# Two graph layers in one kernel: when the second layer's scaled copies and the next batch's preparation are issued

## The chip, the core and the metric

The kernel runs on one core of one Trainium2 chip. The time is the device time of one execution in microseconds (us); several runs are given with their median. One further execution is recorded by the hardware profiler, and all durations below come from that one. PE is the matrix engine (TensorE), PEld its weight loads, DVE is VectorE, ACT is ScalarE, POOL is GpSimd, SP is SyncE, which issues most DMAs.

## The reference

Input `x` is 8 batches of 2048 nodes with 256 features; `adj` is one 2048 x 2048 0/1 matrix for all batches. Two layers run one after the other, each adding to `x`. The change concerns the second:

```python
h = relu(layernorm(x))
q = (h @ W).reshape(B, N, 4, 64)
e_src, e_dst = q . a[:64], q . a[64:]              # per node and head
e = leaky_relu(e_src[:, :, None] + e_dst[:, None, :], 0.2)
attn = softmax(where(adj > 0, e, -9e15), axis=2)   # over the neighbours
x = x + elu(attn @ q)
```

The first layer is multi-head attention under the same mask, with a softmax over each chunk of 256 keys, an output projection and a layer norm. All arithmetic here is in float32.

## The kernel before

One program in five instruction queues, written out in one function, `layers`. Each engine runs its own queue in the order in which the Python code issues to it; semaphores order them against each other, and nothing is rescheduled after that. Small jobs are Python generators: a list `aside` holds them, and `advance()` takes one step from each, until one step gives `None` (a heavy step, one to a call); `True` marks a light step, `False` a wait. `drain(until)` repeats `advance()` until a condition holds.

**The second layer.** A batch has four passes, one for each pair of heads (`hp`) and each half of the 2048 queries (`half`); a pass has 16 rounds, one for each tile of 128 keys (`jt`), so a batch has 64 rounds. Eight batches make 32 passes and 512 rounds. The exponent of the score is taken apart so that no matrix of scores is needed:

- `nears` (L801, ACT), once in a pass: the exponential of the source part for 1024 queries, one tile for each of two heads, into PSUM (`places[0]`, `places[1]`). It reads `es`, fetched by DMA (L593, SP).
- `clipped` (L812, DVE), two instructions a round, one for each head: the larger of near and far part, cut off by the mask, makes a tile `e` of 128 x 1024. `begun` issues it two rounds ahead of its use. Ten `e` tiles exist, two for each of five rounds.
- `weigh_rows` (L823, PE): multiplies `e` by the keys' rows `qn` and adds into `acc`, 8 matmuls a round (the trace shows 16).
- The softmax's denominator takes two key tiles at a time, called pair m here (rounds 2m and 2m+1, m from 0 to 7). In the even round two scaled copies `t` of `e` are made (L926, ACT); in the odd round POOL adds the next `e` onto them (L930), and two rounds later PE sums them (`add_up_rows`, L835) into `den`. The last pair of a pass isn't added by POOL; PE sums `t` and `e` apart, in the same round. Four `t` tiles exist, enough for two pairs.
- At the end of a pass ACT copies `acc` and `den` out (`cT` L935, `dT` L944), and the generator `ending` finishes: PE transposes (`flip`, L156), a reciprocal (L858, DVE), twice a product `z` (L869, DVE), four small ACT instructions (L878 to L881), two POOL adds (L883, L884) and a store.

`den` lies in one half of the PSUM tile `places[2]`; the other half (`aux()`) is the one place in which all small jobs put their PE results.

**The preparation of the next batch** (`preparation`) runs beside the passes of this batch as one more generator: for each of four blocks of 512 nodes it normalises (L144, ACT), transposes (`block_turned`: L156 on PE, the copy `hT` L164 on ACT) and projects onto the two vectors (L620, PE; copy `er` L627, ACT); then come the bounds (L632 to L679 on DVE, ACT and POOL, with two trips through DRAM and some rounds of waiting), and at last eight projections by W (`narrow`, L153, PE, 32 matmuls in the trace for each), each scaled on DVE (L693) into `qn`. Counted by the steps that give `None` there are 21. The passes of the next batch need it, and a `drain` at round 8 of the fourth pass makes sure that it is done.

The order of one round before the change:

```python
ready.append(begun(*rounds[s + 2]))   # nears, if a pass begins there; then e
weigh_rows(jt, hp, now, qn, acc)
# even jt: the two copies t; odd jt: POOL's adds; jt 15: cT
# the sums that are due; jt 15: dT, and ending is put ahead of the others
if jt != NKT - 3:
    advance()
```

## Time and profile before

| | us |
|---|---|
| median of three runs | 4279.99 (4279.74 to 4282.05) |
| the profiled execution: its time | 4285.06 |
| its span, first to last instruction | 4283.3 |
| first `e` of the second layer (L812) | 2761.0 from the start |
| last `e` of the second layer | 4259.1 from the start |
| one L812 / L930 / L926 / L869 | 1.275 / 2.388 / 1.142 / 0.680 |
| granted TensorE clock, mean | 0.993 |

The spans are those of one execution; an instruction's mean comes from its group of equal instructions. Matmuls overlap each other, and their ends are modelled, so the time from the start of one to the start of the next says more of PE than its busy share. A wait in brackets at the end of a line is idle time of the engine just before that instruction, with the instruction that ended it.

### The profile page before, as it was taken

The page shows a single profiled execution, that of the slowest core. Times are in us where ns is not written, and L with a number is a line of the kernel's source. Part 1 is how long each engine was busy: PE and PEld are TensorE (multiplying, and loading weights), DVE is VectorE, ACT ScalarE, POOL GpSimd, SP SyncE. Part 2 cuts the span into 40 slices and gives each one's busy share as a digit, 9 for nine tenths or more (in the row PEclk, how much of TensorE's full clock was granted, in tenths as well). Part 3 has the DMA queues.
Part 4 walks back from the last instruction along what each step waited for, and adds up shares of the span by engine and source line. Part 5 has one row for each costly group of instructions (what it writes and reads, how often), then busy time and mean ns, then how long its engine had stood idle before and what let it go on. Part 6 is the DMA issues. An engine that isn't in the chain of part 4 may idle for free. (4 is left out here: it accounts for less than half of the span.)

```text
span 4283.3 us, 86541 instructions
## 1 busy us (share of the span) xinstructions
PE 4101.6 (96%) x34742; PEld 1478.7 (35%) x34742; DVE 3220.3 (75%) x3974; ACT 2528.9 (59%) x3194; POOL 3411.4 (80%) x1799
## 2 busy tenths in 40 slices
PE   7999999999999999999999989999999999999998
PEld 3333333333333333333333333333333233333322
DVE  5786676766666676666666667789888988888897
ACT  5655565655655555555555557565665656566565
POOL 2577787887887888888788688888788878887897
PEclk9999999999999999999999999999999999999999
DMA  3221111121121111121112122212121211112121
GB/s 110 88 74 56 52 57 52 54 63 46 54 62 47 48 58 57 49 57 59 47 52 59 47 61 61 81 47 67 43 70 35 79 58 57 57 54 70 33 60 36
DMA packets 278730, 248.15 MB, mean 58 GB/s; under 512 B 95792, under 2 KB 228656, under 8 KB 278320
## 3 DMA queue, kind: packets, MB, share of 16 engines
q1 hardware_dynamic: 273136, 223.67, 17.9%
q0 software_dynamic: 5184, 18.88, 1.1%
q8 instruction: 275, 4.51, 0.4%
q14 instruction: 135, 1.11, 0.1%
HBM read 204.15 MB, written 36.18 MB: 56 GB/s over the span
## 5 line engine op out<-in xcount | busy, mean ns | idle before, releaser
L448 DVE SCALAR_TENSOR_TENSOR E<-big,limit 128x1024 f32<-128x1024 f32 x1024 | 1182.2, 1216 | 650.0 <-PE big L440 629.4
L742 POOL TENSOR_TENSOR add<-E 128x1024 f32<-128x1024 f32 x512 | 1203.4, 2372 | 548.2 <-PE both L460 472.2
L454 ACT ACTIVATE E<-E 128x1024 f32<-128x1024 f32 x1024 | 1054.5, 1056 | 535.1 <-DVE E L448 517.1
L812 DVE SCALAR_TENSOR_TENSOR e<-big,far,limit 128x1024 f32<-128x1024 f32 x1024 | 1239.4, 1275 | 37.5 <-POOL t L930 21.0
L930 POOL TENSOR_TENSOR t<-t,e 128x1024 f32<-128x1024 f32 x448 | 1054.6, 2388 | 226.2 <-ACT t L926 219.7
L823 PE MATMUL acc<-e,qn 128*32 128x512 f32 x8192 | 1065.2, 595 | 3.5 <-DVE e L812 3.4
L460 PE MATMUL both<-E,v 128*32 128x512 f32 x8192 | 992.9, 596 | 0.2
L440 PE MATMUL big<-qT,kT 64*128 64x512 f32 x4096 | 964.5, 608 | 28.1 <-DVE E L448 26.5
L926 ACT ACTIVATE t<-e,quot 128x1024 f32<-128x1024 f32 x512 | 562.5, 1142 | 242.4 <-PE big L835 147.5
L440 PEld LDWEIGHTS big<-qT,kT 64*128 64x128 f32 x4096 | 366.0, 187 | 575.3 <-issue 389.5
L500 POOL TENSOR_TENSOR acc<-acc,c 128x1024 f32<-128x1024 f32 x224 | 530.2, 2367 | 1.4 <-DVE c L498 1.4
L460 PEld LDWEIGHTS both<-E,v 128*32 128x32 f32 x8192 | 276.2, 109 | 595.8 <-issue 340.0
L823 PEld LDWEIGHTS acc<-e,qn 128*32 128x32 f32 x8192 | 292.1, 110 | 496.2 <-issue 435.4
L835 PE MATMUL big<-t,for_sums 128*32 128x512 f32 x2048 | 380.3, 596 | 66.7 <-POOL t L930 50.1
L498 DVE TENSOR_TENSOR c<-both,r 128x512 f32<-128x512 f32 x448 | 308.8, 689 | 40.2 <-PE both L460 14.3
L471 PE MATMUL big<-add,ones 128*32 128x512 f32 x2048 | 282.1, 605 | 12.2 <-DVE E L448 1.4
L478 ACT COPY s<-big 128x512 f32<-128x512 f32 x256 | 149.8, 585 | 78.3 <-PE big L471 78.0
L835 PEld LDWEIGHTS big<-t,for_sums 128*32 128x32 f32 x2048 | 80.9, 109 | 279.0 <-POOL t L930 183.3
L153 PE MATMUL big<-w,hT 128*32 128x256 f32 x2048 | 151.1, 380 | 4.1 <-ACT dT L944 4.1
L164 ACT COPY hT<-big 128x512 f32<-128x512 f32 x128 | 74.2, 579 | 132.6 <-PE big L156 132.6
L144 ACT ACTIVATE h<-x,off,rstd 128x256 f32<-128x256 f32 x256 | 139.1, 592 | 14.2 <-DMA x<-x 13.8
L337 ACT ACTIVATE qT<-big,bq 128x512 f32<-128x512 f32 x64 | 43.9, 687 | 148.7 <-PE big L153 148.7
(117 smaller groups left out, 3059.4 us busy)
## 6 DMA issues: line engine op xcount, KB each, us to landing
r<-inv SPq DMA_DIRECT2D x1024, 64.0 KB
x<-in_x_dram SPq DMA_DIRECT2D x96, 512.0 KB
es<-er SPq DMA_DIRECT2D x64, 512.0 KB
adj_in<-in_adj_dram SPq DMA_DIRECT2D x32, 512.0 KB
x<-o POOLq DMA_DIRECT2D x32, 512.0 KB, 3.3
xh<-x SPq DMA_DIRECT2D x64, 256.0 KB
out_dram<-xh SPq DMA_DIRECT2D x64, 256.0 KB
x<-x SPq DMA_DIRECT2D x28, 512.0 KB
```

Of the source, the lines that this page charges most:

```text
L440: nc.tensor.matmul(ps[:, hh, :], ks[kt // NT][own, hp, (kt % NT) * P : (kt % NT + 1) * P], qs[qb][own, hp, :], start=True, stop=True,)
L448: nc.vector.scalar_tensor_tensor(e, ps, -0.5, bcast(limit[:, qb, kt, :], 1, 2), ALU.max, ALU.min)
L454: nc.scalar.activation(e, e, AF.Exp, scale=0.25 * EDGE)
L460: nc.tensor.matmul(both[part][32 * h : 32 * h + 32, :], vs[kt // NT][:, kt % NT, mine], es[h // 2][:, h % 2, :], start=first, stop=not first,)
L498: nc.vector.tensor_tensor(to[:, part, :], both[part], r, ALU.mult)
L500: nc.gpsimd.tensor_tensor(acc, acc, to, ALU.add)
L742: nc.gpsimd.tensor_tensor(both, tiles[0][hp], tiles[1][hp], ALU.add)
L812: nc.vector.scalar_tensor_tensor(e, near[hh], far[:, jt, h : h + 1], limit[:, 2 * half : 2 * half + 2, jt, :], ALU.max, ALU.min,)
L823: nc.tensor.matmul(acc[blk][32 * q : 32 * q + 32, :], qn[jt // NT][:, jt % NT, hp * P + 32 * q : hp * P + 32 * q + 32], es[q // 2][:, blk, :],
L835: nc.tensor.matmul(den[32 * q : 32 * q + 32, :], for_sums[:, m, 2 * hp + q // 2, :], ts[q // 2][:, q % 2, :], start=(m == 0 and k == 0), s ...
L926: nc.scalar.activation(t, now[hh], AF.Copy, scale=quot[:, jt // 2, h : h + 1])
L930: nc.gpsimd.tensor_tensor(ts[hh], ts[hh], now[hh], ALU.add)
```

## The change

Two things change, both in the loop over the second layer's rounds.

The scaled copies move into a function `scaled`, which is called in the odd round for the pair that begins in the next round: after that round's sums (and after `dT` in the last round of a pass) and before `advance()`. The first pair's copies are made ahead of the loop.

The preparation is wrapped in `paced`, which lets a step that gave `None` be followed by the next only when two and a half rounds for each such step have gone by since the preparation began. The `drain` in the fourth pass switches the pacing off.

```diff
+    at, hurry = [0], [False]
+
+    def paced(steps_of):
+
+        first, done = at[0], 0
+        for got in steps_of:
+            yield got
+            if got is None:
+                done += 1
+                while 2 * (at[0] - first) < 5 * done and not hurry[0]:
+                    yield False
...
+    def scaled(k, jt, now):
+
+        b, hp, half = passes[k]
+        quot = shared[b][4]
+        ts = []
+        for hh in range(2):
+            t = heads_tile("t", "q", 4)
+            h = 2 * hp + hh
+            nc.scalar.activation(t, now[hh], AF.Copy, scale=quot[:, jt // 2, h : h + 1])
+            ts.append(t)
+        return ts
...
     ready = [begun(*rounds[0]), begun(*rounds[1])]
+    shares = [scaled(*rounds[0], ready[0])]
...
-        here[0] = len(steps) + s // 4
+        here[0], at[0] = len(steps) + s // 4, s
...
-                aside.append(preparation(b + 1))
+                aside.append(paced(preparation(b + 1)))
...
+            hurry[0] = True
             drain(lambda: b1 in shared)
+            hurry[0] = False
...
         if jt % 2 == 0:
-            ts = []
-            for hh in range(2):
-                t = heads_tile("t", "q", 4)
-                h = 2 * hp + hh
-                nc.scalar.activation(t, now[hh], AF.Copy, scale=quot[:, jt // 2, h : h + 1])
-                ts.append(t)
+            ts = shares.pop()
...
+        if jt % 2 and ready:
+            shares.append(scaled(*rounds[s + 1], ready[0]))

         if jt != NKT - 3:
             advance()
```

## The prediction

> **What bounds the kernel now.** The page first: four engines are all busy, so shares settle nothing.

> ```profile
> PE 4101.6 (96%) x34742; PEld 1478.7 (35%) x34742; DVE 3220.3 (75%) x3974; ACT 2528.9 (59%) x3194; POOL 3411.4 (80%) x1799
> ```

> The diff touches only the second layer, so I cut that into passes by POOL's clock, from the first add (L930) of a pass to the first add of the next: passes 0 to 3 of the fourth batch, then a pass of the last batch, which has no preparation beside it. Columns: stretch, length, then busy PE, PEld, DVE, ACT and POOL.

> ```profile
> 3343.33:3392.92 49.59, 46.09 (x400) 14.81 (x404) 40.44 (x38) 34.34 (x49) 41.49 (x23) 1.00 0.26 79
> 3392.92:3435.62 42.70, 41.45 (x381) 12.63 (x374) 40.85 (x38) 29.66 (x39) 37.96 (x19) 1.00 0.23 55
> 3435.62:3488.54 52.92, 50.79 (x572) 24.06 (x576) 42.80 (x45) 27.37 (x36) 38.48 (x21) 1.00 0.07 21
> 3488.54:3532.32 43.78, 41.87 (x374) 13.24 (x366) 42.70 (x39) 25.94 (x30) 37.96 (x18) 1.00 0.29 82
> 4141.85:4184.47 42.62, 39.92 (x341) 12.31 (x342) 39.85 (x36) 25.95 (x30) 37.88 (x19) 1.00 0.16 51
> ```

> A batch is 189.0 us (the first four rows); the last batch runs at 42.6 a pass. In the last row POOL is busy 37.88 and idle 4.74, nearly all of it one wait, which the timeline at the end of a pass shows.

> ```profile
> 4173.99 2.31 ACT L801 ACTIVATE big<-es,off_s 128x1024 f32<-128x1024 f32 x2 [1.13 <-DVE e L812]
> ...
> 4175.25 0.62 PE L835 MATMUL big<-t,for_sums 128*32 128x512 f32 x2 [0.20 <-POOL t L930]
> ...
> 4182.76 0.58 ACT L944 COPY dT<-big 128x512 f32<-128x512 f32 x1 [2.39 <-PE big L835]
> 4183.24 4.27 ACT L926 ACTIVATE t<-e,quot 128x1024 f32<-128x1024 f32 x4
> ...
> 4184.47 9.43 POOL L930 TENSOR_TENSOR t<-t,e 128x1024 f32<-128x1024 f32 x4 [4.58 <-ACT t L926]
> ...
> 4185.12 0.26 DVE L858 RECIPROCAL inverse<-big 128x16 f32<-128x16 f32 x1 [2.68 <-PE big L156]
> ...
> 4196.34 0.63 ACT L878 ACTIVATE z<-z 128x512 f32<-128x512 f32 x1 [2.18 <-DVE z L869]
> ...
> 4196.46 1.06 PE L835 MATMUL big<-t,for_sums 128*32 128x512 f32 x8 [0.41 <-DVE z L869]
> ...
> 4198.59 2.17 ACT L926 ACTIVATE t<-e,quot 128x1024 f32<-128x1024 f32 x2
> ...
> 4201.14 1.28 POOL L883 TENSOR_TENSOR z<-z 128x512 f32<-128x512 f32 x1
> ```

> The loop that sets 42.6 is POOL's adds (without a break), the PE sums of the last pairs, ACT's copies cT and dT, ACT's first scaled copy, POOL again. DVE has 2.68 us of slack before L858. In passes 0 and 1 the loop is the same: POOL's waits at their ends are 7.62 and 4.58. Pass 2 holds the eight projections (L153, the `qn` steps), and PE sets it: its weighs (L823) start 3.44 apart in a round with a projection where a weigh alone takes 1.72, so a projection costs 1.72; sums (L835) 0.86, four transposes with their turnaround 0.6.

> [...] By start-to-start times PE needs 16 x 1.72 + 9 x 0.86 + 3 x 0.6 = 37.1 of 42.6, so 5 us are free, and I go by those.

> **Part one, copies a round earlier.** No instruction is added; 512 copies (L926, 1.14 each) change place in ACT's queue. A copy writes the `t` tile that pair m-2 held, so it waits for that pair's sums on PE. Before, those sums were issued a round earlier; now they are issued in the same round, just ahead of it, and what follows on ACT waits with it. From the order of the built program, four things follow.

> (a) End of a pass: the copies of pair 7 now stand before the two exponentials (L801) that DVE's next `e` tiles need. Sums of pair 5 resume at 4175.25; elsewhere a copy starts 1.15 after the start of its sums (4208.50 to 4209.65), so second copy 4176.4, exponential 1.05 later at 4177.45, 1.12 long, first `e` of the next pass about 4178.66, not 4175.20: 3.5 late. DVE's slack takes 2.7; six `e` at 1.19 end 4185.9, so L858 and both z (L869) come 0.7 late. POOL's first add waits for the copy behind dT as before, and its `e` is there by 4182.3, two us early: no cost there, and one for one if `e` were later by more than that.

> (b) The second z group (L878 to L881, 1.86 to the end of L880) stood before the copies of pair 3 and now stands behind them. The sums of pair 1 wait for the z in the other half of their PSUM tile (4196.46 above): 4197.16 after. Copies 4198.25 to 4200.4, L880 ends 4202.2, POOL's z 4202.25 instead of 4201.14: POOL stands still 1.1 us a pass. Last batch: 4 x 1.1 = 4.4. [...]

> (c) Passes 0 and 1: the preparation's h and hT (L144 0.59, L164 0.58) now stand behind copies, and PE's transposes, which need them, stand before the next weighs. Pass 0: h of round 5 is ready after sums of pair 1 (end 3358.1) plus copies, z group, two h: 3363.9; PE reaches it at 3359.8 and waits 4.2; two later places (L620 behind an L164 that stands behind copies, and the transposes of round 12) add 0.7 and 1.9. From there to the sums of pair 6 PE needs 10 x 1.72 + 4 x 0.86 + 4 x 0.6 + 0.45 = 23.5, with waits 30.3; POOL needs 27.2, so PE is 3.1 late. Against that, the hT and two h that stood before the first copy of pass 1 (gap 7.62 against 4.58) are gone: -3.0. Pass 0: +0.1, say 0. Pass 1: `e` starts 4.3 before the first add, not 5.8, so (b) becomes 2.6; PE waits 3.1 (L164 behind the second z group) and 1.9 (h behind a copy), and comes 2.3 late to the last sums: +4.9.

> (d) Pass 2: (b) with a lead of 4.6 is 2.3.

> **Part two, pacing.** The order shows what comes of it. Steps counted by weighs before them: projections stood at 40 to 45, 47, 48 and now stand at 45, 47, 48, 51, 52, 54, 55, 56. Transposes move by up to 6 rounds. It is no even spread: fixed waits before the 13th step put it at 42, when the pace is already behind. Nothing is left for the drain at round 56, so no burst; the next passes' loads (L593, SP) are issued at round 56 as before; `x` loads on SP come later by the same few rounds, each still a block of steps ahead of its use. POOL's small L656 and L657 move past z, where DVE's result is ready: 2.06 of wait goes.

> Pass 2 then has two projections before its last sums: two rounds with one need 2 x 1.72 + 0.86 + 1.72 = 6.02 against POOL's two adds 4.78, twice: 2.5 late. 38.5 busy + 4.7 + 2.5 + 0.6 (dT later) + 2.3 (d) = 48.6 for 52.9: -4.3. Pass 3 has six: PE 16 x 1.72 + 9 x 0.86 + 6 x 1.72 + 3 x 0.6 + 1.2 (the first waits for dT) = 48.6 for 43.8: +4.8; POOL's own chain (38 + 4.7 + the z wait) stays inside that.

> Sum per batch: 0 + 4.9 - 4.3 + 4.8 = +5.4. Seven batches have a preparation: 38. The first overlaps the end of layer one, where its PE waits may hide: 0 to 5.4, taken as the others because its passes 2 and 3 get the same order. With 4.4: +42. The profiled execution took 4285.06 (span 4283.3), which becomes 4327; the median of the runs, 4279.99, becomes **4322**.

> **Rivals.** *Faster:* PE's sums are done when ACT reaches the copies. Then (b) and PE's lateness in (c) are nil: pass 0 -3.0, pass 1 0, pass 2 46.3 (-6.6), pass 3 +4.8, so -4.8 x 7 = -34, 4246. For it: POOL's long waits in the second layer are all for a copy (219.7 us), and the 7.62 is cured. Against it: ACT already waits 147.5 us for those sums with a round more in hand. It decides once a copy waits under about a microsecond. *Much slower:* PE sets passes 0 and 1, so its waits count in full (6.8 for 3.1, 5.0 for 2.3): 11.8 a batch, +87, 4367. For it: PE is busy 46.09 of 49.59; against: its sums there wait for POOL. *The pacing does nothing:* pass 2 and 3 keep their old lengths plus 2.3 and 1.1, a batch +8.3, 4342. Against: six of eight projections do leave pass 2. *No change:* POOL's gain at the pass end and the z wait cancel, 4280.

> **How the numbers follow.** Forecast 0.58, much slower or no pacing 0.17, no change 0.07, faster 0.18. About 0.2% (8.6 us) is what a measurement here can tell from nothing. Range 4255 to 4352: down into the faster case, up to between the slower ones. A gain over 8.6 us 0.18, none 0.07, a loss 0.75.

> **What would show it.** The last batch decides (a) and (b) alone: passes of 43.7 instead of 42.6, L883 waiting about 1 us for ACT, the 2.68 before L858 gone and a new DVE wait of 3 to 4 us at L812 for ACT's L801. In pass 1, PE waits at L620 and L156 for ACT's hT and h; pass 2 near 48.6, pass 3 near 48.6. If the last batch stays at 42.6 and passes 2 and 3 add up to under 93, the forecast is wrong and the faster rival holds.

## The result, and the profile after

The changed kernel takes 4348.68 us (median of four runs, 4345.81 to 4350.93) against 4281.02 for the kernel before (4279.74 to 4283.56): a ratio of 1.0157 [1.0139, 1.0175]. The profiled execution took 4345.81 us, 60.8 more than that of before; the medians, over more runs, are 67.7 apart. The copies are L922 now, POOL's adds L952, `cT` L957, `dT` L966; the other lines that matter keep their numbers. First the engine line of the page.

```profile
PE 4107.7 (95%) x34742; PEld 1478.4 (34%) x34742; DVE 3215.8 (74%) x3974; ACT 2524.6 (58%) x3194; POOL 3410.6 (79%) x1799
```

The counts are those of before and the busy times nearly so: no work was added, so all that was lost is waiting. Next the four passes of the fourth batch and one of the last batch, cut by POOL's first add as before (stretch, length, busy PE, PEld, DVE, ACT, POOL, then the granted clock).

```profile
3360.29:3408.43 48.14, 42.04 (x380) 14.52 (x384) 39.24 (x36) 31.85 (x43) 41.47 (x22) 1.00 0.26 77
3408.43:3458.82 50.39, 45.23 (x402) 14.39 (x394) 41.17 (x38) 32.05 (x45) 37.87 (x18) 0.97 0.19 61
3458.82:3508.34 49.52, 43.73 (x412) 15.13 (x416) 41.84 (x44) 27.24 (x36) 38.41 (x21) 1.00 0.10 25
3508.34:3557.90 49.56, 49.54 (x534) 19.81 (x526) 44.06 (x43) 25.64 (x30) 38.05 (x18) 1.00 0.24 63
4196.25:4240.43 44.18, 40.66 (x341) 12.49 (x342) 39.12 (x37) 25.43 (x30) 37.87 (x19) 0.96 0.15 47
```

The batch is 197.6 us for 189.0: pass 0 is 1.5 shorter, pass 1 7.7 longer, pass 2 3.4 shorter, pass 3 5.8 longer. The last batch runs at 44.2 to 44.6 a pass for 42.6. By batches, the first grows by 3.4, the six middle ones by 52.2 together, the last by 8.1; the second layer began 2.9 earlier in this execution, which leaves 60.8. Where the time waits shows in the list of waits (engine, line, what it waited for: us in total, times, longest):

```profile
ACT t L922 <- PE big L835: 293.8, 97, 5.6
...
POOL t L952 <- ACT t L922: 214.1, 38, 11.2
...
POOL z L883 <- ACT z L880: 72.8, 24, 4.8
...
PE big L156 <- ACT h L144: 59.7, 38, 6.6
...
DVE e L812 <- ACT big L801: 56.4, 11, 9.9
```

ACT's copies waited 147.5 us for PE's sums before and now wait 293.8. That alone need cost nothing, ACT being busy 58% of the time; but POOL's wait for the z group (L880) and DVE's for the exponentials (L801) were not among the waits of before, and PE's for `h` was 26.2. (The same list has 83.0 us of DVE's waits before L812 as "issue", for 15.3 before; those too stand at the first `e` of a pass.) All three wait for something that stands behind a copy in ACT's queue. POOL's wait for copies, which an earlier copy could have shortened, is 214.1 for 219.7. The timeline of the last batch shows the order at one end of a pass and in the pass that follows:

```profile
4231.96 2.19 ACT L922 ACTIVATE t<-e,quot 128x1024 f32<-128x1024 f32 x2 [2.10 <-issue]
...
4234.06 2.14 ACT L801 ACTIVATE big<-es,off_s 128x1024 f32<-128x1024 f32 x2
...
4235.24 7.24 DVE L812 SCALAR_TENSOR_TENSOR e<-big,far,limit 128x1024 f32<-128x1024 f32 x6 [5.03 <-issue]
...
4240.43 9.43 POOL L952 TENSOR_TENSOR t<-t,e 128x1024 f32<-128x1024 f32 x4 [5.10 <-ACT t L922]
...
4253.73 1.07 PE L835 MATMUL big<-t,for_sums 128*32 128x512 f32 x8 [1.11 <-DVE z L869]
...
4254.87 2.19 ACT L922 ACTIVATE t<-e,quot 128x1024 f32<-128x1024 f32 x2 [4.59 <-PE big L835]
...
4256.97 0.61 ACT L878 ACTIVATE z<-z 128x512 f32<-128x512 f32 x1
...
4258.84 1.29 POOL L883 TENSOR_TENSOR z<-z 128x512 f32<-128x512 f32 x1 [1.71 <-ACT z L880]
```

The copies of pair 7 end, the exponentials start at once behind them, and DVE has stood still for 5.03 us. (The view puts that wait to "issue", but it ends a moment after the first of the two L801 does.) In the next pass the sums wait for z, ACT waits 4.59 for the sums, and z, which has been ready since about 4253.6, gets its four ACT instructions only from 4256.97 on; POOL stands still for 1.71.

### The profile page after: what moved, and what is told of

Its sections match the earlier page's. It is cut to its first block, busy times and chain, and to the rows that moved or that the text cites. A ratio compares the mean times of both kernels' runs of the same rounds, so it can differ in the third digit from the quotient of the medians.

```text
span 4344.0 us, 86487 instructions
## 1 busy us (share of the span) xinstructions
PE 4107.7 (95%) x34742; PEld 1478.4 (34%) x34742; DVE 3215.8 (74%) x3974; ACT 2524.6 (58%) x3194; POOL 3410.6 (79%) x1799
## 3 DMA queue, kind: packets, MB, share of 16 engines
q14 instruction: 135, 1.11, 0.1%
## 4 chain that ended last, share of the span: by engine, by line
PE 65%; DVE 12%; POOL 11%; issue 7%; ACT 4%; DMA 1%; SPq 0%; POOLq 0%; DVEq 0%; ACTq 0%
PE big L440 19%; PE both L460 18%; PE big L153 12%; DVE e L812 8%; POOL t L952 8%; PE big L471 6%; PE acc L823 6%; PE big L835 2%; PE big L156 1%; POOL add L742 1%; ACT E L454 1%; DVE E L448 1%; ACT t L922 1%; POOL acc L500 1%; DVE z L869 1%
## 5 line engine op out<-in xcount | busy, mean ns | idle before, releaser
L812 DVE SCALAR_TENSOR_TENSOR e<-big,far,limit 128x1024 f32<-128x1024 f32 x1024 | 1239.0, 1274 | 162.1 <-issue 83.0
L952 POOL TENSOR_TENSOR t<-t,e 128x1024 f32<-128x1024 f32 x448 | 1053.1, 2383 | 228.8 <-ACT t L922 214.1
L823 PE MATMUL acc<-e,qn 128*32 128x512 f32 x8192 | 1022.1, 602 | 3.8 <-DVE e L812 3.2
L922 ACT ACTIVATE t<-e,quot 128x1024 f32<-128x1024 f32 x512 | 564.0, 1143 | 480.8 <-PE big L835 293.8
L823 PEld LDWEIGHTS acc<-e,qn 128*32 128x32 f32 x8192 | 283.6, 110 | 511.0 <-issue 436.1
L835 PE MATMUL big<-t,for_sums 128*32 128x512 f32 x2048 | 307.0, 600 | 66.7 <-POOL t L952 32.4
L498 DVE TENSOR_TENSOR c<-both,r 128x512 f32<-128x512 f32 x448 | 308.8, 689 | 40.3 <-PE both L460 14.7
L835 PEld LDWEIGHTS big<-t,for_sums 128*32 128x32 f32 x2048 | 77.3, 111 | 244.0 <-issue 158.4
L156 PE MATMUL big<-ident,h 128*128 128x128 f32 x512 | 94.5, 298 | 61.7 <-ACT h L144 59.7
L144 ACT ACTIVATE h<-x,off,rstd 128x256 f32<-128x256 f32 x256 | 139.0, 592 | 14.2 <-DMA x<-x 13.8
L883 POOL TENSOR_TENSOR z<-z 128x512 f32<-128x512 f32 x64 | 82.3, 1286 | 80.7 <-ACT z L880 72.8
L153 PE MATMUL big<-w,hT 128*32 128x256 f32 x2048 | 125.3, 380 | 5.0 <-ACT dT L966 4.9
```

Of the source, the lines that this page charges most:

```text
L153: nc.tensor.matmul(to[j : j + 32], lhsT[:, j : j + 32], rhs, start=start, stop=stop)
L812: nc.vector.scalar_tensor_tensor(e, near[hh], far[:, jt, h : h + 1], limit[:, 2 * half : 2 * half + 2, jt, :], ALU.max, ALU.min,)
L823: nc.tensor.matmul(acc[blk][32 * q : 32 * q + 32, :], qn[jt // NT][:, jt % NT, hp * P + 32 * q : hp * P + 32 * q + 32], es[q // 2][:, blk, :],
L922: nc.scalar.activation(t, now[hh], AF.Copy, scale=quot[:, jt // 2, h : h + 1])
L952: nc.gpsimd.tensor_tensor(ts[hh], ts[hh], now[hh], ALU.add)
```

## The experiments

The theory: the loss comes from the place of the copies in ACT's queue, right behind PE's sums of the same round, where their wait is handed on to the z group, the exponentials, `h` and `hT`; the pacing by itself is a small gain. The rivals blame the pacing, the mere delay of the exponentials, or PE's clock. Pass lengths are read from POOL's first add of a pass to that of the next, a batch is four of them, "last batch" its passes.

**Copies earlier, no pacing.**

```diff
-                aside.append(paced(preparation(b + 1)))
+                aside.append(preparation(b + 1))
```

> The copies a round earlier, the preparation not paced. Theory Q (ACT's queue: a copy now stands directly behind the sums that free its tile, and what stands behind it waits): passes of the last batch 44.4 us as in the changed kernel (42.6 before); passes 0 and 1 together 98 to 100 (92.3 before); pass 2 52.9 + 2.3 = 55.2; pass 3 43.8 + 1.8 = 45.6; a batch 199, in all +70 us, ratio about 1.016. Rival P (the pacing lost the time, the copies are neutral): a batch 189 to 190, ratio 1.000 to 1.003, last batch 42.6.

4367.29 us, ratio 1.0198 [1.0182, 1.0214]. Batches 199.3 to 202.7 us, last batch 43.7 to 44.0. The copies alone cost 84 us, more than the whole change and more than the 70 expected: that the pacing lost the time is refuted.

**Pacing, copies in their old place.**

```diff
-            ts = shares.pop()
+            ts = scaled(k, jt, now)
...
-        if jt % 2 and ready:
-            shares.append(scaled(*rounds[s + 1], ready[0]))
...
```

> The preparation paced, the copies in their old round. Theory Q: last batch 42.6; passes 0 and 1 as before, 92.3; pass 2 38.5 + 4.7 + 2.5 + 0.6 = 46.3; pass 3, held by PE's six projections, 47 to 48.6; a batch 186 to 187.5 against 189.0, in all -10 to -20 us, ratio 0.995 to 0.998. Rival P: a batch of 194 or more, ratio above 1.008.

4273.44 us, ratio 0.9977 [0.9968, 0.9986]: a gain of 10 us. The same four passes of the fourth batch here:

```profile
3337.09:3385.58 48.49, 44.78 (x388) 13.96 (x388) 40.43 (x37) 31.79 (x44) 41.52 (x23) 1.00 0.25 82
3385.58:3428.97 43.39, 42.49 (x393) 14.07 (x390) 39.85 (x36) 31.90 (x44) 37.94 (x19) 1.00 0.17 51
3428.97:3474.63 45.66, 42.52 (x412) 15.00 (x416) 40.62 (x42) 27.40 (x36) 38.45 (x22) 1.00 0.10 27
3474.63:3524.87 50.24, 50.23 (x533) 19.00 (x526) 45.88 (x44) 25.72 (x30) 38.12 (x19) 1.00 0.28 75
```

187.8 for 189.0 us, and the last batch, which has nothing to pace, stays at 42.6. Pass 2 gains 7.3, pass 3 gives 6.5 back: it holds six projections, and PE is busy for all of it. Beside the changed kernel's fourth batch, the copies' move costs 7.0 in pass 1 (1.7 of it by the half clock described below, which falls into pass 0 in other batches) and 3.9 in pass 2; passes 0 and 3 are 0.4 and 0.7 shorter with it.

**The copies of pair 7 back in their old round** (the others early, pacing on), so that the exponentials stand ahead of them again.

```diff
-            ts = shares.pop()
+            ts = shares.pop() if shares else scaled(k, jt, now)
...
-        if jt % 2 and ready:
+        if jt % 2 and jt != NKT - 3 and ready:
```

> The whole change, but the copies of pair 7 stay in their old round, behind the two exponentials of the next pass. Theory Q: DVE's wait of 5 us for the exponentials is gone and its 2.7 us before the reciprocal are back; POOL's wait for the second z group falls from 1.7 to about 0.5, because the z itself comes earlier: last batch 43.1; a batch 195 to 196 instead of 197.6; in all 12 to 18 us under the changed kernel, ratio to before about 1.012. If the exponentials' delay were the main cause (rival A), the last batch is 42.6 and a batch under 191, ratio below 1.004.

4316.96 us, ratio 1.0082 [1.0066, 1.0097]; batches 193.6 to 195.1, last batch 43.0, 43.0, 43.6. DVE no longer waits for L801 in the last batch, and the 3.1 us before L858 are back. One pair of eight is worth 32 us, more than the 12 to 18 expected, but not all of the loss.

**The copies behind the small steps of the round**, all of them early.

```diff
+        if jt != NKT - 3:
+            advance()
         if jt % 2 and ready:
             shares.append(scaled(*rounds[s + 1], ready[0]))
-
-        if jt != NKT - 3:
-            advance()
```

> The whole change, but the copies are issued behind the round's small steps and not ahead of them, still in the odd round. Theory Q: the second z group, h and hT stand ahead of the copies again, so POOL waits for no z group and PE for no h or hT behind a copy; last batch 42.6 to 42.8; pass 0 49.6, pass 1 42.7 to 44, pass 2 46.3 to 47, pass 3 48.6; a batch 187 to 189, ratio 0.996 to 1.001. Rival A (the exponentials' delay, which is still there): last batch 44 or more, a batch above 193, ratio above 1.008.

4285.10 us, ratio 1.0004 [0.9995, 1.0013]: no change. Batches 189.7; in the last batch the passes are 42.6, POOL's end-of-pass wait is 4.58, and L883 does not wait. The copies are as early on ACT relative to the rounds as in the change, and only what a round's small steps issue to ACT goes ahead of them. DVE's waits for L801 are still there, 2.1 to 2.9 us a pass in the last batch, and cost nothing there.

In the middle batches this order is not free: beside the pacing alone (187.8 us, ratio 0.9977) a batch is 1.9 longer. Pass 1 is 1.0 longer, pass 2 1.6 longer (47.27 for 45.66) and pass 3 0.7 shorter. The end of pass 2 in the fourth batch shows its part:

```profile
3478.13 1.92 PE L835 MATMUL big<-t,for_sums 128*32 128x512 f32 x16 [1.44 <-DVE qn L693]
...
3482.68 2.39 POOL L952 TENSOR_TENSOR t<-t,e 128x1024 f32<-128x1024 f32 x1 [8.71 <-ACT t L922]
```

DVE's first `e` of the next pass waits 2.75 us for the exponentials, the scaling of a projection (L693) stands behind it in DVE's queue, and PE's last sums wait 1.44 for that scaling. POOL's wait at this place is 8.71 here and in the change, but 7.05 with the pacing alone and 7.04 with pair 7 in its old place, where DVE does not wait for the exponentials. So their delay is free in the last batch and costs 1.7 us in pass 2; what lengthens pass 1 was not taken apart. Between the change and the pacing alone lie 1.8% (1.0157 and 0.9977); this order leaves 0.3% of them, and the rest is lost when the copies stand ahead of a round's small steps.

**Three pairs of `t` tiles in the last batch**, with the change as it is elsewhere. Two tiles that are idle there take every third pair, so a copy waits for sums three pairs back.

```diff
-            t = heads_tile("t", "q", 4)
+            third = b == B - 1 and (8 * k + jt // 2) % 3 == 2
+            t = heads_tile("t", *(("x", 3) if third else ("q", 4)))
```

> The changed kernel, but in the last batch the scaled copies rotate over six tiles (three pairs) instead of four; the two extra tiles are idle there. A copy then waits for sums three pairs back instead of two. Theory (the copies, placed behind PE's sums of the same round, hold up what stands behind them in ACT's queue): the wait is gone, so the last batch's passes go from 44.2 to 44.6 back to 42.6 or, since the first copy of a pass no longer waits for pair 6 either, down to 40.5; POOL's waits at L883 (1.05 to 1.80) and DVE's waits for L801 (3.9 to 5.0) in the last batch fall under 0.3 and 1. The other batches stay at 197 to 199 us. Rival (it is the place of the copies in ACT's queue as such, 2.3 us of work ahead of the z group and the exponentials, not the wait in front of them): the passes stay at 43.7 or more and L883 still waits 1 us or more.

One execution, 4334.48 us. The middle batches are those of the change (197.0 to 198.5); in the last one the passes are 42.60, 42.65 and 42.67. Its timeline:

```profile
4191.07 9.44 POOL L953 TENSOR_TENSOR t<-t,e 128x1024 f32<-128x1024 f32 x4 [4.58 <-ACT t L923]
...
4201.22 2.34 ACT L923 ACTIVATE t<-e,quot 128x1024 f32<-128x1024 f32 x2 [1.60 <-DVE e L812]
...
4203.47 0.61 ACT L878 ACTIVATE z<-z 128x512 f32<-128x512 f32 x1
...
4207.78 1.28 POOL L883 TENSOR_TENSOR z<-z 128x512 f32<-128x512 f32 x1
```

The order in ACT's queue is that of the change, the copies of pair 3 and then the second z group; but the copies wait for DVE's `e` (1.60) and no longer for PE, the z group begins 12.4 us after POOL's first add instead of 16.5 (4240.43 to 4256.97 above), and POOL's L883 starts without a wait; DVE no longer waits for the exponentials either. So in the last batch it is the wait in front of the copies, not their place as such. The pass did not go below 42.6, because the first copy still stands behind `dT` (4.58 again). Three pairs in every batch were not tried, nor was a `den` in a tile of its own apart from the small jobs'.

**PE kept busy in its new gaps.** The change, with eight matmuls of zero weights behind weigh 6 of passes 0 and 1.

```diff
...
         weigh_rows(jt, hp, now, qn, acc)
+        if jt == 6 and k % 4 < 2 and b + 1 < B:
+            for blk in range(2):
+                for q in range(4):
+                    nc.tensor.matmul(
+                        acc[blk][32 * q : 32 * q + 32, :], zeros, now[q // 2][:, blk, :], start=False, stop=False
+                    )
...
```

> The change, with eight extra matmuls of zero weights (added into acc, 1.72 us of PE by start-to-start times) in passes 0 and 1 of each batch with a preparation, right behind weigh 6, where PE otherwise stands still for 3.3 us (pass 0, for h) and 2.6 us (pass 1, for hT). Theory (a stretch in which PE hardly works is followed by 3.4 us at half the granted clock, and that is what makes pass 0 or 1 of a batch 1.0 to 2.5 us longer than its clean form): the granted clock reads 1.00 in passes 0 and 1 of the middle batches, they come to 48.1 to 48.3 and 48.7 to 48.9, the batch to 196 to 196.5 for 197.6 on average; passes 2, 3 and the last batch are as in the change, and the total falls by 6 to 12 us. Rival (the low clock is a mere by-product, PE has time to spare there): the clock reads 1.00 and the passes stay at 98.5 to 99.3 together. Second rival (PE sets these passes in full, so that 1.72 us of extra matmuls cost 1.72 us each): the two passes come to 100 or more.

The reason for it is a thing in the profile after that the prediction did not have: the granted clock. In the last-batch pass above that reads 0.96, these are the stretch just before the clock falls and the one in which it is low:

```profile
4217.92:4221.33 3.41, 1.05 (x4) 0.14 (x4) 3.41 (x4) 1.12 (x1) 3.41 (x3) 1.00 0.69 202
4221.33:4224.74 3.41, 3.37 (x16) 0.79 (x20) 3.41 (x4) 1.17 (x2) 3.41 (x2) 0.50 0.02 7
```

In the first PE is busy for 1.05 us only, waiting for POOL's adds, and all through the second its clock is granted at one half (0.50), so that PE loses 1.7 us, half of 3.41. Every pass of the second layer reads 1.00 before; after, one or two passes of each batch read 0.93 to 0.97, and which of them changes from batch to batch. (The runs with the copies alone and with pair 7 in its old place have such passes too, at 0.93 to 0.97; in those with the pacing alone and with the copies behind the small steps every pass reads 1.00.) The extra matmuls gave 4339.05 us, ratio 1.0125 [1.0108, 1.0142], 10 us less than the change although PE does more (`zeros` is a tile of zeros, so nothing is added to `acc`). The two ratios' intervals just touch; of the 8.6 us between the profiled executions, 5.8 lie in the six middle batches and 2.5 ahead of the second layer. Passes 0 and 1 of the third and the fourth batch, and pass 1 of the last:

```profile
3158.48:3206.62 48.14, 43.83 (x396) 15.52 (x400) 39.25 (x36) 31.85 (x43) 41.52 (x22) 1.00 0.23 72
3206.62:3255.32 48.70, 45.24 (x418) 14.65 (x410) 41.18 (x38) 32.05 (x45) 37.90 (x18) 1.00 0.18 62
3354.42:3404.26 49.84, 45.15 (x396) 15.30 (x400) 39.25 (x36) 31.85 (x43) 41.43 (x23) 0.97 0.23 68
...
4187.91:4231.60 43.69, 39.61 (x341) 12.27 (x342) 39.74 (x37) 25.64 (x30) 37.88 (x18) 1.00 0.16 49
```

In the rows at 1.00, pass 0 is 48.14 and pass 1 48.70, to a hundredth what the change has in most of its own undisturbed passes; at 0.97, pass 0 is 49.84: 1.70 more, half of 3.4. Pass 1 is now at full clock in all six middle batches, pass 0 in three (PE still waits about 1.5 for `h` in all of them). In the last batch, where nothing was added, the slow stretch happened to stay away from passes 1 and 2, and they are 43.7 instead of 44.2 and 44.6, with L883 waiting 1.1. So the clock is no mere by-product: in these passes it costs 1.7 us a time. Middle batches: 195.3 to 197.6.

**Only the copies between the passes early** (pair 0, behind `dT`; pacing on).

```diff
-            ts = shares.pop()
+            ts = shares.pop() if jt == 0 else scaled(k, jt, now)
...
-        if jt % 2 and ready:
+        if jt == NKT - 1 and ready:
```

> The changed kernel with the earlier copies only at the end of a pass (pair 0 of the next pass, behind dT and ahead of the small steps); pairs 1 to 7 are copied in their old round. Theory (the loss lies in the copies inside the pass; the one between passes only gains, by passing the preparation's h and hT): last batch 42.6 a pass, no wait of DVE for L801, batch 184 to 188, ratio 0.990 to 0.998. Rival (the copies between the passes cost as well, because they stand ahead of the preparation's steps): batch over 190, ratio over 1.000.

4266.20 us, ratio 0.9964 [0.9951, 0.9978]; batch 186.8, last batch 42.6, clock 1.00. This part of the change does not lose: pass 0 is 1.0 shorter than with the pacing alone, and the other passes are the same.

**The copies of pair 0 ahead of `dT`**, all others in their old round, with the pacing and without.

```diff
-            ts = shares.pop()
+            ts = shares.pop() if jt == 0 else scaled(k, jt, now)
...
+        if jt == NKT - 1 and ready:
+            shares.append(scaled(*rounds[s + 1], ready[0]))
         if jt == NKT - 1:
             dT = const.tile([P, QB], F32, tag="wk", name="dT")
             nc.scalar.copy(dT, den)
...
-        if jt % 2 and ready:
-            shares.append(scaled(*rounds[s + 1], ready[0]))
```

> The pacing of the change, the copies in their old places, but for the first pair of a pass: its two copies are issued in round 15 of the pass before, behind the sums and ahead of dT instead of behind it. They need only the sums of pair 6, while dT needs those of pair 7 as well. Theory: what closes POOL's loop at the end of a pass is adds, sums, ACT, first copy, adds; with dT out of it POOL's 4.58 becomes about 2.5, a pass without preparation goes from 42.6 to 40.6 (DVE's busy 39.85 is the next floor), and the preparation's passes gain 2 each, 3 more where h and hT stood before the first copy: batch 187.8 becomes 177 to 183, ratio 0.977 to 0.991. Rival (DVE or PE is right behind POOL): the passes stay at 42 or more, ratio 0.995 to 0.999.

> As the kernel with the first pair's copies ahead of dT, but the preparation is not paced. Theory: last batch 40.6 a pass, batches with a preparation 189 less 5 to 10, ratio 0.979 to 0.992; pacing is worth as much beside it as without it, about 0.002. Rival (the projections of pass 2 were bound by PE and stay so, the others by DVE): ratio 0.995 or more.

With the pacing 4240.63 us, ratio 0.9905 [0.9890, 0.9920]; without 4248.10, ratio 0.9925 [0.9911, 0.9939]. Batches 184.5 and 185.5, both a little above what was expected, last batch 40.3 to 41.0; the pacing is worth 0.0020 here and 0.0023 without this order. The timeline of the paced one in the last batch:

```profile
4139.84 2.19 ACT L922 ACTIVATE t<-e,quot 128x1024 f32<-128x1024 f32 x2
...
4141.07 7.07 POOL L952 TENSOR_TENSOR t<-t,e 128x1024 f32<-128x1024 f32 x3 [2.77 <-ACT t L922]
4141.93 0.58 ACT L968 COPY dT<-big 128x512 f32<-128x512 f32 x1
```

POOL's 4.58 is 2.2 to 2.8, as the copy no longer waits for the sums of pair 7. DVE is busy 39.85 of that 41.0 us pass, so it is next.

**Four projections in pass 2 and four in pass 3**, with that order of copies and with the old one.

```diff
-                while 2 * (at[0] - first) < 5 * done and not hurry[0]:
+                while done > 14 and at[0] - first < 2 * done + 11 and not hurry[0]:
```

> The first pair's copies ahead of dT, as before, and another pace: the first 14 heavy steps of the preparation go as fast as without pacing, the projections behind them at one per two rounds, so that four stand in pass 2 (behind weighs 40, 41, 44, 47) and four in pass 3 (48, 51, 52, 54); the pace of the change puts two in pass 2 and six in pass 3. Theory (a projection costs PE 1.72, a pass without preparation leaves PE some 3.5 free, so a clump overflows and an even share overflows less): passes 2 and 3 come to 37.1 + 4 x 1.72 = 44.0 each, 44 to 46 with small waits, against 44.1 and 51.2; passes 0 and 1 stay at 45.2 and 43.9; batch 176 to 181 for 184.5, ratio 0.977 to 0.986. Rival (what counts is the number of projections in a batch, not their place): batch stays at 184 or more, ratio 0.990.

> The same pace, four projections in pass 2 and four in pass 3, with all copies in their old places. Theory: passes 2 and 3 at 45 to 47 each for 52.9 and 43.8 before, and for 45.65 and 50.24 with the pace of the change; passes 0 and 1 as before, 49.6 and 42.7; batch 183 to 186, ratio 0.988 to 0.995. Rival: 187.8 as with the pace of the change, ratio 0.998.

4240.10 us, ratio 0.9902 [0.9887, 0.9917], and 4273.45 us, ratio 0.9979 [0.9970, 0.9988]: each the same as with the pace of the change. Passes 2 and 3 are 47.0 and 48.2 (for 44.1 and 51.2), so the even share moved time and saved none. That theory fell. The timeline of pass 3, which begins at 3458.81, shows one reason:

```profile
3460.32 1.93 PE L153 MATMUL big<-w,hT 128*32 128x256 f32 x32 [0.69 <-ACT dT L968]
3462.39 0.69 DVE L693 TENSOR_TENSOR qn<-big,share 128x512 f32<-128x512 f32 x1 [3.76 <-PE big L153]
3467.19 4.73 POOL L952 TENSOR_TENSOR t<-t,e 128x1024 f32<-128x1024 f32 x2 [3.67 <-DVE e L812]
```

The projection right behind a pass's end waits for `dT`, its scaling on DVE waits for it ahead of the next `e`, and POOL runs dry.

**None in a pass's first round.**

```diff
-                while done > 14 and at[0] - first < 2 * done + 11 and not hurry[0]:
+                while done > 14 and (at[0] - first < 2 * done + 11 or at[0] % NKT == NKT - 1) and not hurry[0]:
```

> The kernel with four projections in pass 2 and four in pass 3, but none in the first round of a pass: the one behind weigh 48 moves, so that pass 3 holds those behind 51, 52, 54, 55. Before, the projection right behind dT writes the tile of the small jobs while ACT still copies dT from its other half; its product L693 stands in DVE's queue ahead of the next e, waits 3.76, and POOL then waits 3.67 for e. Theory: this one wait is what made pass 3 longer than the sum (48.2 for 44 to 46); without it pass 3 is 44.5 to 45.5, pass 2 stays at 47, batch 180 to 182 for 184.2, ratio 0.983 to 0.987. Rival (any projection costs its 1.7 to 2 us wherever it stands): pass 3 stays at 47.5 or more, ratio 0.990.

4227.96 us, ratio 0.9874 [0.9857, 0.9890]: the best version, 1.3% faster than before and 2.8% faster than the change. Pass 3 is 46.4, batch 182.4; the two waits of 3.7 are gone, but only 1.8 us came back, for PE is now busy through the whole pass (46.42 of 46.42); theory and rival each held half.

## Why the prediction was right, point by point

The sign, the mechanism and the range held: 4348.68 lies between 4255 and 4352, but only 3 us under the upper end, which had been set for the slower rivals. The size came out short: +42 us were forecast, and the profiled executions differ by 60.8, the medians by 67.7.

- **(a), end of a pass.** DVE's wait for L801 was to be 3 to 4 us with the 2.68 before L858 gone: it is 3.92 where the clock is full, 5.03 and 4.80 after a slow stretch, and the 2.68 is gone. That it costs nothing by itself was right in the last batch by the copies behind the small steps, up to 2.9 us; in pass 2 the delay costs 1.7, which the prediction had at nothing.
- **(b), the z group.** L883 was to wait 1.1 us and the pass to be 43.7. In the last batch of the kernel with extra matmuls, passes 1 and 2 at full clock are 43.7 and the wait 1.1. Behind a pass with a slow stretch it is 1.7, and 1.8 in the batch's first pass, which follows one with projections. The third pair of tiles takes all of it away, which shows the mechanism. The sums do wait for the z in the other half of their tile (1.11 us at 4253.73 above), as the forecast had it. The last batch was to lose 4.4 us and lost 8.1.
- **(c), passes 0 and 1.** 49.6 and 47.6 were forecast, together 97.2. The undisturbed passes are 48.14 and 48.70, together 96.8: the sum came out right by luck, for pass 0 is 1.5 shorter than forecast (the pacing itself shortens it by 1.1, which the prediction had not seen) and pass 1 1.1 longer. PE's waits for `h` and `hT` were to be 4.2 and 3.1 and are 3.3 and 2.6. But each middle batch has a pass at 0.93 to 0.97, and the pair takes 97.8 to 99.3.
- **(d) and pass 2.** L883 waits 2.25 for 2.3 forecast. POOL's wait at the end is 8.7 for 4.7 + 2.5 + 0.6 = 7.8, so the pass is 49.5 for 48.6. The runs account for it: 45.66 with the pacing alone (46.3 forecast), 2.25 for z and 1.7 for the exponentials' delay make 49.6.
- **Part two, pass 3.** PE was to set it at 48.6. PE does set it (busy 49.54 of 49.56), at 49.6: the sum of PE's work was 1.0 short. The pacing by itself, -6.6 + 4.8 = -1.8 a batch in the forecast, is -1.2.
- **The first batch** was taken as the others, at 5.4, and lost 3.4.

The mis-sized term is thus (c) with pass 2 and 3: +5.4 a batch forecast, +8.7 measured on the mean of the six middle ones (52.2 / 6). Of the 3.3 missing, the undisturbed batch (48.14 + 48.70 + 49.52 + 49.56 = 195.9) accounts for 1.5: passes 2 and 3 came 0.9 and 1.0 longer, passes 0 and 1 together 0.4 shorter. The rest, 1.8, is the half clock: PE's waits were costed as standing still only, and not for what comes after them.

Of the rivals, *faster* needed sums that are done when ACT reaches the copies; ACT waited twice as long for them as before (293.8 us for 147.5). *Much slower* had PE's waits count in full; with the half clock some do, and the result lies between it and the forecast. *The pacing does nothing* is refuted: pass 2 is 7.3 shorter with it. *No change* is what the copies behind the small steps give, not this kernel.

## What to carry to other kernels

Moving an instruction earlier on an in-order engine can move its wait as well (ACT's copies waited 147.5 us for PE's sums before and 293.8 after): before it is done, list what stands behind the new place and who waits for that, and move only those whose input is ready there. Here one pair of copies in eight gained 0.75% when it was put ahead of an instruction that waited longer, while moving the other seven cost 1.9% (1.0157 for 0.9964). When a change makes PE wait, look at the granted clock slice by slice, for the gap can be followed by slow matmuls, which cost 1.7 us here behind a stop of 2.57, at a granted clock of 0.50 for 3.41 us.

## What the runs showed of the hardware

In the trace of the changed kernel, six of the slow stretches of 3.41 us begin at 2985.70, 3183.68, 3429.43, 3825.38, 4023.35 and 4221.33. They are 197.98, 245.75, 395.95, 197.97 and 197.98 us apart, which is 58, 72, 116, 58 and 58 times 3.4133 us (the 1235.63 us from the first to the last, divided by 362). PE was busy for 0.83 to 1.48 of the 3.41 us ahead of each of them. Divided into lengths of 3.41 us, one of which ends where the slow stretch at 3429.43 begins, the stops in passes 0 and 1 of the fourth batch read:

```profile
3374.82:3378.23 3.41, 1.68 (x16) 0.42 (x8) 3.41 (x4) 3.38 (x5) 3.33 (x3) 1.00 0.26 77
3378.23:3381.64 3.41, 1.83 (x16) 0.82 (x20) 3.41 (x4) 2.88 (x6) 3.41 (x3) 1.00 0.00 0
...
3426.02:3429.43 3.41, 0.84 (x24) 0.50 (x24) 3.41 (x4) 2.83 (x6) 1.38 (x2) 1.00 0.00 0
```

The stop of 3.26 us falls across two of these lengths, in which PE was busy for 1.68 and 1.83 of 3.41 us, and the clock stayed at 1.00. The one of 2.57 lies inside one of them, with 0.84 busy, and the next ran at 0.50. That the same stop slows one batch and not another by where it falls is an estimate from these two; no run shows it. The busy time, whose ends are modelled, does not part the cases: in other lengths of the same row, 1.41 us busy left the clock at 1.00 (3968.73 to 3972.14), while 1.48 did not (3180.27 to 3183.68), nor did 1.79 in the kernel with extra matmuls (the 3.41 us ahead of its slow stretch, from 3371.52).
